# Loading the head of a two-layer kernel in other pieces: second chunk in halves, later x behind it, ten zero matmuls

## The chip, the cores and the metric

The kernel runs on one core of one Trainium2 chip. The metric is the device time of one execution in microseconds (us). Engines are called as the profile calls them: PE is TensorE (PEld its weight loads), DVE VectorE, ACT ScalarE, POOL GpSimd, SP the engine that issues most DMA transfers. All times in this document are us unless marked ns.

## The reference

Eight samples of 256 rows by 1024 features go through two residual layers:

```python
# layer 0: one weight for all, plus a +-1 mask per sample, scaled by a coefficient per sample
output = jnp.einsum('bsi,oi->bso', hidden_states, W) + b
sign = (2 * mask - 1).astype(hidden_states.dtype)
diff = jnp.einsum('bsi,bio->bso', hidden_states, sign)
y = x + output + diff * coeff[:, None, None]
# layer 1: a weight per sample, chosen by id among eight
out = y + jnp.einsum('bsi,boi->bso', y, weight[adapter_ids])
```

x is (8, 256, 1024) in float32, the mask (8, 1024, 1024) in int32, the eight layer-1 weights (8, 1024, 1024) in float32. Since coeff multiplies a whole sample, layer 0 of a sample is one product with the matrix W.T + coeff * (2 * mask - 1).

## The kernel before

**Stages.** One stage is one layer of one sample, in the order (layer, sample) = (0,0), (1,0), (0,1), (0,2), (1,1), (0,3), (1,2) and so on to (1,7). The first stage is called the head. All others compute their 1024 x 1024 product by seven half-size products p1 to p7 (a Winograd scheme, table `PRODUCTS`) on quarter blocks named 11, 12, 21, 22. They need sums of activation blocks (s1 to s4) and of weight blocks (t1 to t4), which DVE makes (`sum_of`, L542 and L559). TensorE's order is p1, p5, p6, p2, p7, p3, p4. p5 multiplies s1 with t1, p6 multiplies s2 with t2, p7 multiplies s3 with t3, p4 uses t4. DVE adds the products into the result (`add`, L672). In a layer-0 stage ACT scales each mask block (L515) and DVE adds W to it (L529, the fold). For a layer-1 stage the result of layer 0 is transposed: DVE transposes 32 x 32 squares (L439) and ACT moves them into place (`move`, L453, 32 moves a sample).

**The head** works otherwise, since no data is there yet. It takes the contraction in eight chunks k of 128 rows. For each chunk SP loads mask0[k] (L283, 128 x 1024, 512 KB) and w0T[k] (L287, the same size); ACT scales the mask (L301), DVE adds w0T to it (L309, the fold), and TensorE multiplies, into four PSUM tiles `first[j, h]`, with column half j of the output (L316, one matmul for each 128 output columns, 256 wide, two records each in the profile). x comes in pairs of chunks (`load_x0`, L274): 256 KB a pair. DVE evicts the four tiles with x and the bias added (L343); that is the input of the next stage, which is computed with weights as the left operand (`flipped`, L598). Stages after that use L608.

What is loaded in one go is a piece. `pieces` lists them: chunk 0 in two column halves, the other chunks whole. `load_w0` puts x of chunks 0 and 1 behind the first piece, of chunks 2 and 3 behind chunk 1, of chunks 4 to 7 behind chunk 2. `parts` says in what spans of columns a piece is scaled and folded: the first piece in quarters of a row's 1024 columns, chunk 1 in halves, others whole. The matmuls of a piece wait only for the span that they read. The last two chunks are multiplied by column half: chunks 6 and 7 for j = 0, then for j = 1, so that half of the output can be evicted sooner.

**What sets the order.** Each load, scale, fold, group of matmuls, sum and addition is a `Task` with an engine, an expected length and what it comes after. `plan` runs a list schedule over these lengths, and each engine's program is written in the order of the planned starts. The lengths of the head's scales and folds follow from `length` (0.4 for the first piece, 0.75 for chunk 1, 1.22 for the others). All head transfers go through SP's one queue in the order of their issue.

**Before the tasks** (L797 to L810), TensorE multiplies zeros: eight matmuls 128 x 512 in bfloat16 into a tile that nobody reads. After the fifth, one small matmul spreads the coefficients over the partitions, and DVE makes c2_sb and cn_sb of them, which the scales use.

Of the kernel before, what the change touches and what calls it, by code (L numbers as in the profile page):

```python
# [14 lines left out]
P = 128  # L15
# [126 lines left out]
def kernel(  # L142
# [26 lines left out]
    nc = tc.nc  # L169
    B = coeff.shape[1]  # L170
    _, _, _, KH, TH = xT.shape
    NL, _, _, _, H = w1T.shape
    KC, D = 2 * KH, 2 * H
# [35 lines left out]
    zeros = const.tile([P, H], BF16, name="zeros")  # L209
# [10 lines left out]
    def task(*args, **kw):  # L220
        tasks.append(Task(*args, **kw))
        return tasks[-1]

    def take(r: Buffer):
        count[0] += 1
        r.tile = pools[r.pool].tile(shapes[r.pool], F32, tag=r.pool, name=f"{r.pool}_{count[0]}")
        return r.tile
# [30 lines left out]
    first = {(j, h): Buffer("ps") for j in range(2) for h in range(2)}  # L258
    xb = Buffer("r")
    half = KH // 2  # L260
    pieces = [(0, ds(0, H)), (0, ds(H, H))] + [(k, ds(0, D)) for k in range(1, KC)]
    w0_rows = w0_sb.rearrange("p k j n -> p k (j n)")

    def x0_view():
        flat = x0.tile.rearrange("p q k n -> p (q k n)")[:, 0 : KC * 2 * TH]
        return flat.rearrange("p (k n) -> p k n", k=KC)
# [5 lines left out]
    def load_x0(lo: int, hi: int, queue):  # L272
        pairs = slice(lo // 2, hi // 2)
        queue.dma_start(  # L274
            out=x0_view()[:, lo:hi].rearrange("p (g k) n -> p g (k n)", k=2),
            in_=x0T[pairs].rearrange("g p n -> p g n"),
        )

    def load_mask(n: int):
        k, cols = pieces[n]  # L280
        if m[k // 2].tile is None:
            take(m[k // 2])
        nc.sync.dma_start(out=m_view(k)[:, cols].bitcast(I32), in_=mask0[k][:, cols])  # L283

    def load_w0(n: int):
        k, cols = pieces[n]
        nc.sync.dma_start(out=w0_rows[:, k, cols], in_=w0T[k][:, cols])  # L287
        if n in (0, 2, 3):
            load_x0(*{0: (0, 2), 2: (2, KH), 3: (KH, KC)}[n], nc.sync)

    def parts(n: int):

        k, cols = pieces[n]
        size = {0: 2 * P, 2: H}.get(n, cols.size)
        return k, [ds(at, size) for at in range(cols.start, cols.start + cols.size, size)]

    def scale_first(n: int):
        k, spans = parts(n)
        for cols in spans:
            t = m_view(k)[:, cols]  # L300
            nc.scalar.activation(  # L301
                t, t.bitcast(I32), AF.Identity, bias=cn_sb[:, 0:1], scale=c2_sb[:, 0:1]
            )

    def fold_first(n: int):
        k, spans = parts(n)
        for cols in spans:
            t = m_view(k)[:, cols]
            v.tensor_tensor(t, t, w0_rows[:, k, cols], ALU.add)  # L309
# [43 lines left out]
    for n, (k, cols) in enumerate(pieces):  # L353
        share = cols.size / D
        opens = opened != k // 2
        length = {0: 0.4, 2: 0.75}.get(n, 1.22 * share)
        ld = task(
            "DMA",
            1.32 * share,
            lambda n=n: load_mask(n),  # L360
            takes=[m[k // 2]] if opens else [],
            uses=[] if opens else [m[k // 2]],
            latency=1.5,
            latest=0.2 * n,
        )
        ld2 = task(
            "DMA", 1.32 * share, lambda n=n: load_w0(n), latency=1.5, latest=0.2 * n + 0.1
        )
        sc = task("ACT", length, lambda n=n: scale_first(n), after=[ld], uses=[m[k // 2]])
        fo = task("DVE", length, lambda n=n: fold_first(n), after=[sc, ld2], uses=[m[k // 2]])  # L370
        folded.append(fo)
        last_scale = sc
        opened = k // 2
        if n == 0:
            tasks[0].takes = [x0] + list(tasks[0].takes)
            tasks[0].uses = [x0] + list(tasks[0].uses)
            x0.users += 1
# [91 lines left out]
    def stage(s: int):  # L469
# [66 lines left out]
        def sum_of(what: str, after=()):  # L536
# [24 lines left out]
            for n, rows in enumerate(parts):  # L561
                t = task(
                    "DVE",
                    BLOCK / len(parts),
                    lambda rows=rows: emit(rows),
                    after=[done[left], done[right], done.get(what), *after],
                    takes=[W[what]] if fresh and n == 0 else [],
                    uses=src + ([W[what]] if fresh and n else []),
                )
                if fresh and n == 0:  # L570
                    t.stage = s
                done[what] = t
# [222 lines left out]
    with tc.manual_schedule():  # L795
        take(x0)
        nc.scalar.dma_start(out=c_row, in_=coeff)  # L797
        v.memset(zeros, 0.0)
        v.memset(ones, 1.0)
        v.memset(warm, 0.0)  # L800

        nc.scalar.activation(warm, warm, AF.Identity, bias=warm, scale=1.0)
        idle = pools["ps"].tile([P, H], F32, tag="ps", name="idle")
        c_ps = pools["ps"].tile([P, B], F32, tag="ps", name="c_ps")
        for n in range(8):
            nc.tensor.matmul(out=idle, lhsT=zeros[:, 0:P], rhs=zeros, start=True, stop=True)
            if n == 4:
                nc.tensor.matmul(out=c_ps, lhsT=ones, rhs=c_row, start=True, stop=True)
                v.tensor_scalar(c2_sb, c_ps, 2.0, None, ALU.mult)
                v.tensor_scalar(cn_sb, c_ps, -1.0, None, ALU.mult)  # L810
        for t in plan(tasks, room, may_take):
            t.emit()
            if t is folded[0]:

                v.memset(ids_sb, 0)
                v.memset(b_sb, 0.0)
                nc.gpsimd.dma_start(out=ids_sb, in_=ids)
                nc.gpsimd.dma_start(out=b_sb, in_=biasT)
# [58 lines left out]
```

## Time and profile before

| what | value |
|---|---|
| time, median of 3 runs | 404.0 us (403.77 to 405.08) |
| the profiled execution's own time | 404.47 us |
| its span, first to last instruction | 402.7 us |
| PE busy | 396.5 us, 98% of the span |
| DVE busy | 330.5 us, 82% |
| ACT busy | 183.5 us, 46% |
| granted TensorE clock, mean | 0.999 |
| moved by DMA | 102.99 MB, mean 256 GB/s |

A group's line in the profile names the source line, the engine, the operation, what is written and read with its shape, the number of instructions, and then busy time, the mean ns of one and the idle time ahead of them with what ended it. A timeline's row has the start, the duration, the engine and the same names, and in brackets the idle time of that engine just before. "SPq" rows are issues of transfers, not the transfers themselves. w is any weight tile, a any activation tile, r a row tile of results, ps a PSUM tile, w_sb the copy of W. In the changed kernel a line stands one lower in the file than in the kernel before (L316 becomes L317), from L803 on some more.

### The profile page before, as it was taken

The numbers are of one execution on the slowest core, as the hardware profiler recorded it, in microseconds if no ns is written. First come the engines' busy times: TensorE is split into PE (matmuls) and PEld (weight loads), VectorE is DVE, ScalarE is ACT, GpSimd is POOL, SyncE is SP. The second block draws the span as 40 slices with busy tenths as digits, with TensorE's granted clock in tenths as the row PEclk, the third lists the DMA queues.
The fourth block names the chain that finished last, engine by engine and source line by source line (L and its number), as shares of the span: only waits on it lengthen the run. The fifth ranks groups of instructions, "written<-read, shape, count | busy, mean of one in ns | idle before, by whom it ended". The sixth has DMA issues, their size and how long they took to land.

```text
span 402.7 us, 3428 instructions
## 1 busy us (share of the span) xinstructions
PE 396.5 (98%) x1154; PEld 201.8 (50%) x1154; DVE 330.5 (82%) x306; ACT 183.5 (46%) x303; POOL 27.2 (7%) x44
## 2 busy tenths in 40 slices
PE   8899999999999999999999999999999999999996
PEld 5689995444444444444444444444444444444443
DVE  2347999999999999799968998789977999668242
ACT  3461735205952396880069610894119920391000
POOL 1000111100011100011010100102001020001101
PEclk9999999999999999999999999999999999999999
DMA  7999999982696828958399583987659694701102
GB/s 268 408 413 422 422 335 400 380 293 107 251 343 194 357 104 341 335 164 319 111 401 304 187 336 112 370 255 282 239 200 338 194 365 157 281 33 53 53 0 105
DMA packets 18564, 102.99 MB, mean 256 GB/s; under 512 B 2226, under 2 KB 2482, under 8 KB 9074
## 3 DMA queue, kind: packets, MB, share of 16 engines
q1 hardware_dynamic: 13952, 87.23, 55.9%
q0 software_dynamic: 4448, 15.47, 14.4%
q8 instruction: 9, 0.15, 0.1%
q14 instruction: 9, 0.07, 0.1%
q10 hardware_dynamic: 146, 0.07, 0.1%
HBM read 94.38 MB, written 8.39 MB: 255 GB/s over the span
## 4 chain that ended last, share of the span: by engine, by line
PE 92%; DMA 4%; DVE 2%; issue 1%; SPq 0%; DVEq 0%
PE ps L608 84%; PE ps L598 5%; DMA w_sb<-w0T 4%; PE ps L316 4%; DVE w L559 1%; DVE a L343 0%; DVE w L309 0%; SPq L283 0%; DVE a L542 0%; SPq L274 0%; SPq L287 0%; DVE r L757 0%; DVEq L343 0%; DVEq L309 0%
## 5 line engine op out<-in xcount | busy, mean ns | idle before, releaser
L608 PE MATMUL ps<-w,a 128*128 128x512 f32 (+1 forms) x792 | 336.7, 588 | 0.0
L608 PEld LDWEIGHTS ps<-w,a 128*128 128x128 f32 x792 | 149.9, 190 | 186.7 <-issue 183.4
L559 DVE TENSOR_TENSOR w<-w,w 128x2048 f32<-128x2048 f32 (+1 forms) x61 | 136.8, 2252 | 3.0 <-PE ps L608 2.5
L453 ACT ACTIVATE a<-turn 32x256 f32<-32x256 f32 x224 | 92.7, 414 | 68.5 <-DVE turn L439 65.7
L672 DVE TENSOR_TENSOR r<-r,ps 128x512 f32<-128x512 f32 x73 | 49.1, 680 | 24.9 <-PE ps L608 24.6
L529 DVE TENSOR_TENSOR w<-w,w_sb 128x2048 f32<-128x2048 f32 x28 | 63.9, 2286 | 5.7 <-ACT w L515 5.7
L515 ACT ACTIVATE w<-w,cn_sb,c_sb 128x2048 f32<-128x2048 int32 x28 | 58.5, 2091 | 15.7 <-DMA w<-mask 15.3
L542 DVE TENSOR_TENSOR a<-a 128x512 f32<-128x512 f32 x59 | 39.4, 686 | 0.3
L644 ACT ACTIVATE s<-ps 128x512 f32<-128x512 f32 x15 | 8.9, 591 | 63.2 <-PE ps L608 54.0
L316 PE MATMUL ps<-a,w 128*128 128x256 f32 x128 | 30.5, 399 | 1.1 <-DVE w L309 1.0
L698 POOL DMA_DIRECT2D out<-r x31 | 17.0, 550 | 190.1 <-DVE r L672 190.0
L316 PEld LDWEIGHTS ps<-a,w 128*128 128x128 f32 x128 | 25.3, 201 | 6.8 <-DVE w L309 3.2
L644 ACT ACTIVATE u<-ps 128x512 f32<-128x512 f32 x15 | 8.9, 595 | 39.2 <-PE ps L608 38.8
L309 DVE TENSOR_TENSOR w<-w,w_sb 128x1024 f32<-128x1024 f32 (+2 forms) x11 | 10.2, 934 | 15.2 <-DMA w_sb<-w0T 12.8
L598 PE MATMUL ps<-a,w 128*128 128x128 f32 x192 | 22.0, 276 | 0.2 <-DVE a L542 0.2
L598 PEld LDWEIGHTS ps<-a,w 128*128 128x128 f32 x192 | 21.8, 192 | 0.5 <-DVE a L542 0.4
L418 POOL DMA_DIRECT2D r<-bias x7 | 8.7, 1245 | 173.9 <-DMA r<-xR 173.9
L439 DVE STREAM_TRANSPOSE turn<-r 128x512 f32<-128x512 f32 x28 | 19.8, 708 | 0.6
L301 ACT ACTIVATE w<-w,cn_sb,c_sb 128x1024 f32<-128x1024 int32 (+2 forms) x11 | 10.9, 1004 | 14.6 <-DMA w<-mask 13.1
L672 DVE TENSOR_TENSOR r<-r,s 128x512 f32<-128x512 f32 x14 | 9.6, 684 | 6.6 <-ACT s L644 6.6
L672 DVE TENSOR_TENSOR r<-r,u 128x512 f32<-128x512 f32 x14 | 9.6, 686 | 3.4 <-ACT u L644 3.4
L343 DVE TENSOR_TENSOR a<-ps,r 128x512 f32<-128x512 f32 x4 | 2.7, 688 | 3.2 <-PE ps L316 3.2
(27 smaller groups left out, 24.8 us busy)
## 6 DMA issues: line engine op xcount, KB each, us to landing
w<-w1T SPq DMA_DIRECT2D x32, 1024.0 KB, 8.4
w<-mask SPq DMA_DIRECT2D x28, 1024.0 KB, 10.0
out<-r POOLq DMA_DIRECT2D x31, 256.0 KB, 7.4
r<-xR SPq DMA_DIRECT2D x7, 1024.0 KB, 8.0
a<-xT SPq DMA_DIRECT2D x7, 1024.0 KB, 9.2
r<-bias POOLq DMA_DIRECT2D x7, 1024.0 KB, 15.7
w<-mask SPq DMA_DIRECT2D x7, 512.0 KB, 9.9
w_sb<-w0T SPq DMA_DIRECT2D x7, 512.0 KB, 10.2
```

Of the source, the lines that this page charges most:

```text
L316: nc.tensor.matmul(out=t.rearrange("p (c n) -> p c n", c=half)[:, c % half], lhsT=m_view(k)[:, ts(oc, P)], rhs=x0_view()[:, k], start=k == ...
L439: lambda t=t, opens=not turned: v.transpose(out=(take(r) if opens else r.tile)[:, t], in_=view(source.tile)[:, 2 * t + j]),
L453: nc.scalar.activation(to[:, :, :, f], src[:, :, :, g], AF.Copy)
L515: nc.scalar.activation(t, t.bitcast(I32), AF.Identity, bias=cn_sb[:, b : b + 1], scale=c2_sb[:, b : b + 1])
L529: lambda q=q: v.tensor_tensor(W[q].tile, W[q].tile, w0[q], ALU.add),
L542: lambda: v.tensor_tensor(part(what), part(left), part(right), op),
L559: v.tensor_tensor(to[:, rows], a, c, op)
L598: nc.tensor.matmul(out=t[:, ts(c, TH)], lhsT=W[w].tile[:, k, ts(c, P)], rhs=part(a)[:, k], start=opens and c == 0 and k == 0, stop=k == KH ...
L608: nc.tensor.matmul(out=t[:, cols], lhsT=part(a)[:, k], rhs=W[w].tile[:, k, cols], start=opens and k == 0, stop=k == KH - 1, skip_group_che ...
L644: lambda: nc.scalar.activation(take(r), bank.tile, AF.Copy),
L672: v.tensor_tensor(to, left, get(r), op)
L698: lambda: (queue or nc.gpsimd).dma_start(out=out0[:, block(q)] if flipped else out[b - 1, :, int(q[0]) - 1, lo:hi], in_=R[b].tile[:, block ...
```

## The change

Chunk 1 is loaded in two column halves, as chunk 0 is, so there is one piece more. x of chunks 2 and 3 stays behind chunk 1, now behind its second half; x of chunks 4 to 7 goes behind chunk 3 instead of chunk 2. `parts` and `length` have an entry for one piece beside the first; its number goes from 2 (then chunk 1) to 4 (now chunk 2), so that chunk 1's halves are scaled and folded one by one as they come, and chunk 2 is scaled and folded in two halves. In `plan`'s input a half of chunk 1 has half of 1.22, chunk 2 has 0.75. Ahead of the head TensorE multiplies zeros ten times, the last two 256 and 128 columns wide.

```diff
-    pieces = [(0, ds(0, H)), (0, ds(H, H))] + [(k, ds(0, D)) for k in range(1, KC)]
+    pieces = [(k, ds(j * H, H)) for k in range(2) for j in range(2)]
+    pieces += [(k, ds(0, D)) for k in range(2, KC)]
...
     def load_w0(n: int):
         k, cols = pieces[n]
         nc.sync.dma_start(out=w0_rows[:, k, cols], in_=w0T[k][:, cols])
-        if n in (0, 2, 3):
-            load_x0(*{0: (0, 2), 2: (2, KH), 3: (KH, KC)}[n], nc.sync)
+        if n in (0, 3, 5):
+            load_x0(*{0: (0, 2), 3: (2, KH), 5: (KH, KC)}[n], nc.sync)
...
-        size = {0: 2 * P, 2: H}.get(n, cols.size)
+        size = {0: 2 * P, 4: H}.get(n, cols.size)
...
-        length = {0: 0.4, 2: 0.75}.get(n, 1.22 * share)
+        length = {0: 0.4, 4: 0.75}.get(n, 1.22 * share)
...
-        for n in range(8):
-            nc.tensor.matmul(out=idle, lhsT=zeros[:, 0:P], rhs=zeros, start=True, stop=True)
+        for n, size in enumerate((H, H, H, H, H, H, H, H, 2 * P, P)):
+            nc.tensor.matmul(
+                out=idle[:, 0:size], lhsT=zeros[:, 0:P], rhs=zeros[:, 0:size], start=True, stop=True
+            )
             if n == 4:
```

Here P is 128, H 512, D 1024, KH 4 and KC 8.

## The prediction

> **What bounds the kernel now.** I read the page's busy row first, then the chain that ended last, then the timelines of TensorE, the DMA queue and VectorE over the first 47 us.
>
> The page's first row and, from the chain in order of time (start us, us, what), its pieces after 18 us:
>
> ```profile
> PE 396.5 (98%) x1154; PEld 201.8 (50%) x1154; DVE 330.5 (82%) x306; ACT 183.5 (46%) x303; POOL 27.2 (7%) x44
> ...
> 7.49 10.63 DMA w_sb<-w0T
> 18.22 1.24 DVE w L309
> 19.50 14.10 PE ps L316 x64
> ...
> 40.08 0.70 DVE a L542
> 40.83 21.70 PE ps L598 x192
> 62.53 336.52 PE ps L608 x792
> ```
>
> TensorE runs without a break from 40.83 to 399.05. So only two things shorten the run: TensorE reaching 40.83 earlier, and nothing later running out because of it. Ahead of that the chain is a transfer (chunk 3 of w0T, issued at 7.49, landed by 18.12), its fold, and matmuls. TensorE's timeline, with idle time in brackets:
>
> ```profile
> 5.49 5.54 PE L316 MATMUL ps<-a,w 128*128 128x256 f32 x16
> 11.81 7.50 PE L316 MATMUL ps<-a,w 128*128 128x256 f32 x32 [0.78 <-DVE w L309]
> 19.50 17.53 PE L316 MATMUL ps<-a,w 128*128 128x256 f32 x80 [0.19 <-DVE w L309]
> 36.87 3.73 PE L598 MATMUL ps<-a,w 128*128 128x128 f32 x32
> 40.83 10.98 PE L598 MATMUL ps<-a,w 128*128 128x128 f32 x96 [0.22 <-DVE a L542]
> ```
>
> A chunk is 16 records. From 19.50 to 36.87, 80 records take 17.37: 0.216 each, and 0.10 more for the first after a wait; a chunk is 3.45. The 32 records at 36.87 go at 0.112 each (21.70 / 192 = 0.113), so TensorE could have gone on at 40.44 and not at 40.83: 0.39 lost, plus 0.10 for the restart. The idle column understates these waits, since ends are modelled.
>
> The DMA queue of SP. Its waits are landings: an issue stands until the transfer eight before it has landed, so each start here dates a landing:
>
> ```profile
> 12.95 0.33 SPq L287 DMA_DIRECT2D w_sb<-w0T  x1
> 14.23 0.33 SPq L283 DMA_DIRECT2D w<-mask  x1
> 15.58 0.33 SPq L287 DMA_DIRECT2D w_sb<-w0T  x1
> 16.86 0.33 SPq L283 DMA_DIRECT2D w<-mask  x1
> 18.14 0.33 SPq L287 DMA_DIRECT2D w_sb<-w0T  x1
> ```
>
> In order these are the landings of mask 2, w0T 2, x of chunks 4-7, mask 3, w0T 3. VectorE's folds start with them (14.30, 18.22), ScalarE's scales too (12.95, 16.87). The head is bound by the order and the bytes of this queue until TensorE, at 3.45 a chunk against 2.56 of transfer, falls behind it at 19.50.
>
> VectorE between head and stage 1:
>
> ```profile
> 33.69 0.69 DVE L343 TENSOR_TENSOR a<-ps,r 128x512 f32<-128x512 f32 x1 [0.17 <-PE ps L316]
> 34.29 4.55 DVE L559 TENSOR_TENSOR w<-w,w 128x1024 f32<-128x1024 f32 x3
> 38.76 1.28 DVE L343 TENSOR_TENSOR a<-ps,r 128x512 f32<-128x512 f32 x2
> 40.08 0.69 DVE L542 TENSOR_TENSOR a<-a 128x512 f32<-128x512 f32 x1
> ```
>
> The three L559 are t1 in halves and t3. t3 (2.29) stands ahead of the last two evictions and s1, and s1 is what p5 waits for at 40.83.
>
> **The change, part by part.**
>
> (1) Chunk 1 in halves. Two transfers of 512 KB become four of 256 KB, with rows of 2 KB instead of 4 KB. Two more issues on SP at 0.43 each: SP is far ahead of the data (w0T 3 is issued at 7.49 and lands at 18.12), so they cost nothing; without that cover, 0.9. Eight transfers in flight now hold fewer bytes, but near 9.7 still 2.75 MB (three of 256 KB, four of 512 KB), at 512 KB in 1.28 some 7 us of work: the engines don't run dry. The rows cost something: 512 KB of x in 2 KB rows took 15.58 - 14.23 = 1.35, 512 KB in 4 KB rows 1.28. So +0.07 per 512 KB, and chunk 1 (1 MB) delays all behind it by 0.14. [...] TensorE is through with chunk 0 at about 11.1; the first half of chunk 1 is folded by about 10.4 (w0T 1 landed by 11.0, less two transfers of 0.65), the second by 11.9, so chunk 1 ends near 14.7, ahead of chunk 2 and not a bound.
>
> (2) Chunk 2 is now the one that is scaled and folded in halves (size table of `parts`). Its first fold starts at 14.30 + 0.14 = 14.44. Chunk 1 shows today what a half is worth: fold at 11.06, matmul at 11.81, 0.75 later. So chunk 2 begins at 15.19 instead of 15.58. The second half follows 0.61 later, when TensorE has 1.8 of work. ScalarE's extra instruction (0.81 and about 0.7 against 1.24) ends before w0T 2 lands.
>
> (3) x of chunks 4-7 moves behind chunk 3: 1.35 earlier for chunk 3, less 0.14. Fold 18.22 - 1.21 = 17.01, matmul 19.50 - 1.21 = 18.29. TensorE is on chunk 2 until 15.19 + 0.10 + 3.45 = 18.74, so no wait. That x now lands at about 18.3, and is read from 22.2.
>
> (4) What is late next: chunk 4, whose bytes are only delayed by the 0.14. Fold 20.78 + 0.14 = 20.92, matmul 1.28 later, 22.20. TensorE is done with chunk 3 at 18.74 + 3.45 = 22.19: a dead heat. Before, it came to chunk 4 at 19.50 + 0.10 + 3.45 = 23.05. The head gains 0.85. Chunks 5-7 are folded 0.9 and more ahead of TensorE. Stage 1 starts at 36.02 instead of 36.87.
>
> (5) The order. SP's and POOL's lists are as before outside the head. The planner, fed the new lengths, puts t3 behind s1, t2, s2 and one addition on VectorE. First evictions 0.85 earlier, at 31.97 and 32.83; t1 needs the second w1 block (landed 33.45, now 33.59), so t1 runs 33.63 to 36.0; evictions 35.9 and 36.5, s1 37.1 to 37.8. p5 is wanted at 36.02 + 3.57 = 39.59: the wait of 0.39 + 0.10 goes, with 1.8 to spare. t2 and s2 end at 40.0 and 40.7, p6 begins at 43.2; t3 ends near 43.5, p7 begins at 50.3.
>
> (6) Two short zero matmuls (and two weight loads beside them). Cold ones of 512 columns are spaced 0.43, so these take 0.21 and 0.11. Today the eighth leaves TensorE free at 5.22, and 5.49 is the fold; now free at about 5.55. 0.06 later, covered by the 0.78 of waiting at 11.81. What they do to the clock is not in the trace. The first eight records of L316 take 634 ns each, those from 9.4 on 379:
>
> ```profile
> L316 PE MATMUL ps<-a,w x8: 634/634/767, 5.5 to 8.6; 128*128 128x256 f32 x8
> ...
> L316 PE MATMUL ps<-a,w x7: 379/379/380, 9.4 to 10.6; 128*128 128x256 f32 x7
> ```
>
> Full speed came 3.7 us after 5.49. An earlier release gains nothing, chunk 2's data being the bound. [...]
>
> **Sum.** 0.85 + 0.49 = 1.34 us less.
>
> **Does the rest follow?** TensorE comes 1.34 earlier to everything after 41 us. VectorE is nearly full from 33 to 100 us and gains less at once, but it waits 0.9 for TensorE at 69.44, which absorbs that. In the next stretch the new order puts the addition of p7 ahead of a fold and waits about 0.6 for it; from there it is some 0.8 ahead. The tightest place is the second layer of the second sample at 110.44: ScalarE's moves (L453) end at 109.42, a margin of 1.0. Now 108.6 against 109.1: 0.5 left. p5 and p6 of the stage at 86.4 have over 1 us each. If this cover goes, part of 1.34 is given back, not more.
>
> The profiled execution took 404.47, span 402.7, so 1.8 lies outside; it stands 0.5 above the median of 404.0, within their spread of 403.77 to 405.08. I take the 1.34 off the median: 402.7.
>
> **Rivals.** *(a) Part of it only.* If the half of chunk 2 doesn't let TensorE start, chunk 2 begins at 15.72 and the head gains 0.33, in all 0.82: 403.2. If p5 still waits, 0.85: 403.15. [...] If the moves at 109 are late by more than 0.5, the same sort of size. For: the dead heat in (4). Against: the row of chunk 1, and 1.8 of spare time for s1.
> [...]
> *(c) Nothing arrives.* If some wait later had bound TensorE anyway, 404.0; the unbroken 358 us speak against it.
>
> **Numbers.** What a measurement of this kernel can tell from no change is about 0.3%, 1.2 us; 402.8 is the border. The forecast is 0.68 (its own range 402.2 to 403.1; 0.58 of it beyond the border, 0.10 short of it), (a) and (c) together 0.20 (0.02 beyond the border), (b) and other losses 0.12. So faster 0.60, same 0.28, slower 0.12. The range 401.9 to 404.2 takes in (a), (c), and leaves out most of (b).
>
> **What would show it.** Span about 401.4. L316 after the first 32 records without a pause from 15.2; chunk 2's first fold near 14.4; chunk 3's near 17.0; L598 starting near 36.0, and no gap ahead of its second 32; L608 starting near 61.0. Wrong if chunk 2's fold comes past 15.2, if L316 pauses near 22, or if L608 shows a wait near 109.

## The result, and the profile after

| | before | after |
|---|---|---|
| median | 404.2 us (403.77 to 405.08, 7 runs) | 402.83 us (402.45 to 403.55, 7 runs) |
| ratio, 95% interval | | 0.9963 (0.9952 to 0.9975) |
| profiled execution, its span | 404.47, 402.7 us | 403.55, 401.8 us |

The changed kernel is faster by 1.5 us (404.2 x 0.0037), with an interval of 1.0 to 1.9; the medians lie 1.37 apart. The predicted time was 402.7. The execution that was profiled is the slowest of the seven (their spans go from 400.7 to 401.8), so its trace shows less of the gain than the median has: 0.9 of span.

The page of the changed kernel, its busy row and the chain that ended last (start us, us, what):

```profile
PE 396.2 (99%) x1156; PEld 202.5 (50%) x1156; DVE 330.9 (82%) x307; ACT 183.8 (46%) x304; POOL 27.2 (7%) x44
...
1.68 4.84 DMA a<-x0T
6.52 0.14 issue
6.65 30.12 PE ps L317 x128
36.77 25.01 PE ps L599 x224
61.78 336.52 PE ps L609 x792
```

No fold and no DVE step is left in the chain. It is one transfer, the first pair of x, and from 6.65 on nothing but TensorE. The last piece has the same 336.52 as before, so all that was gained lies ahead of it. TensorE's timeline:

```profile
3.97 1.78 PE L807 MATMUL idle<-zeros 128*128 128x512 bf16 x5
6.65 30.12 PE L317 MATMUL ps<-a,w 128*128 128x256 f32 x128 [0.90 <-DMA a<-x0T]
36.61 14.46 PE L599 MATMUL ps<-a,w 128*128 128x128 f32 x128
```

Before, the 128 head records stood in three rows with waits at 11.81 and 19.50; now they are one row. Stage 1 starts at 36.61 (36.87 before), and its p5 follows p1 without a gap: 128 records in one row, where before 32 and 96 stood apart. p5 starts at 36.61 + 3.57 = 40.18 (40.83 before). The head gave 0.26, the wait of p5 0.39, its restart 0.10: 0.75, and stage 2 starts at 61.62 instead of 62.37. What else the span lost, 0.14, lies behind TensorE's last matmul.

SP's queue. The waiting issues date landings: the first three those of a mask half, a w0T half and a mask half, the last five those of mask 2, w0T 2, mask 3, w0T 3 and x of chunks 4 to 7, in this order:

```profile
7.28 0.33 SPq L288 DMA_DIRECT2D w_sb<-w0T  x1
7.92 0.33 SPq L284 DMA_DIRECT2D w<-mask  x1
8.57 0.33 SPq L288 DMA_DIRECT2D w_sb<-w0T  x1
...
12.64 0.33 SPq L288 DMA_DIRECT2D w_sb<-w0T  x1
13.92 0.33 SPq L284 DMA_DIRECT2D w<-mask  x1
15.20 0.33 SPq L288 DMA_DIRECT2D w_sb<-w0T  x1
16.48 0.33 SPq L284 DMA_DIRECT2D w<-mask  x1
17.83 0.33 SPq L288 DMA_DIRECT2D w_sb<-w0T  x1
```

Chunk 2 landed at 13.92 (14.23 before), chunk 3 at 16.48 (18.14 before). VectorE, from the fold of chunk 2 on:

```profile
14.02 1.29 DVE L310 TENSOR_TENSOR w<-w,w_sb 128x512 f32<-128x512 f32 x2 [2.56 <-DMA w_sb<-w0T]
16.56 1.23 DVE L310 TENSOR_TENSOR w<-w,w_sb 128x1024 f32<-128x1024 f32 x1 [1.25 <-DMA w_sb<-w0T]
20.47 1.22 DVE L310 TENSOR_TENSOR w<-w,w_sb 128x1024 f32<-128x1024 f32 x1 [2.68 <-DMA w_sb<-w0T]
...
34.04 2.35 DVE L560 TENSOR_TENSOR w<-w,w 128x1024 f32<-128x1024 f32 x2
36.30 1.28 DVE L344 TENSOR_TENSOR a<-ps,r 128x512 f32<-128x512 f32 x2
37.62 0.69 DVE L543 TENSOR_TENSOR a<-a 128x512 f32<-128x512 f32 x1
...
41.64 2.28 DVE L560 TENSOR_TENSOR w<-w,w 128x2048 f32<-128x2048 f32 x1
```

The two halves of t1 at 34.04, the last two evictions, s1 at 37.62; t3 only at 41.64. s1 was at 40.08 before, behind t3.

Why did so early data give the head only 0.26? Two rows of the records of L317 (how many; least, median and largest duration in ns; from when to when):

```profile
L317 PE MATMUL ps<-a,w x10: 634/634/765, 6.7 to 10.6; 128*128 128x256 f32 x10
```

```profile
L317 PE MATMUL ps<-a,w x116: 379/379/471, 11.1 to 36.0; 128*128 128x256 f32 x116
```

TensorE started late, at 6.65, since the first x landed at 6.52 (5.36 before), and its first ten records went at the slow clock (634 ns each; by the trace's clock record full speed came at 11.2). The trace has the starts of slow records 0.427 apart and those of fast ones 0.216, so the head can be written as a sum: start + 128 x 0.216 + 0.211 for each slow record + the rest. Here 6.65 + 27.65 + 2.11 + 0.20 = 36.61. The rest is what the first three terms leave over: the waits, with 0.10 for each restart after one and about 0.13 that the first record takes longer. Here no wait is left in it, and the end is set by the start and the clock. The same sum over every profiled execution of this study (kernels as told below; stage 1 is the end of the sum; p5 less stage 1 is 3.57 where p5 does not wait):

| kernel | first matmul | slow records | rest (waits) | stage 1 starts | p5 less that |
|---|---|---|---|---|---|
| before | 5.49 | 8 | 2.04 | 36.87 | 3.96 |
| after | 6.65 | 10 | 0.20 | 36.61 | 3.57 |
| e1_t3_late | 7.00 | 9 | 0.20 | 36.74 | 3.57 |
| e2_x_only | 5.46 | 10 | 0.60 | 35.82 | 5.00 |
| e3_halves_only | 6.72 | 0 | 2.20 | 36.57 | 3.57 |
| e4_eight_zeros | 5.99 | 12 | 0.14 | 36.31 | 3.57 |
| e5_x_and_t3 | 5.46 | 4 | 2.00 | 35.95 | 3.57 |
| e6_after_t3_early | 5.46 | 0 | 2.64 | 35.75 | 4.83 |
| e7_x_first | 7.26 | 8 | 0.12 | 36.71 | 3.57 |
| e8_x_act | 5.69 | 0 | 2.13 | 35.47 | 3.57 |
| e9_chunk2_whole | 6.41 | 0 | 2.04 | 36.10 | 3.57 |
| e10_thirds_x_act | 5.64 | 9 | 0.29 | 35.48 | 3.57 |
| e11_few_zeros | 5.20 | 13 | 0.19 | 35.79 | 3.57 |
| e12_thirds_few_zeros | 5.68 | 14 | 0.12 | 36.40 | 3.57 |

Rows with a rest of 2 us and more are bound by the data, rows with 0.1 to 0.3 by TensorE's own start and clock; e2, with 0.60, stands between.

### The profile page after: what moved, and what is told of

Read it like the earlier page. It is cut to its first block, busy times and chain, and to the rows that moved or that the text cites. A ratio compares the mean times of both kernels' runs of the same rounds, so it can differ in the third digit from the quotient of the medians.

```text
span 401.8 us, 3435 instructions
## 1 busy us (share of the span) xinstructions
PE 396.2 (99%) x1156; PEld 202.5 (50%) x1156; DVE 330.9 (82%) x307; ACT 183.8 (46%) x304; POOL 27.2 (7%) x44
## 4 chain that ended last, share of the span: by engine, by line
PE 97%; DMA 1%; SPq 0%; issue 0%; DVE 0%
PE ps L609 84%; PE ps L317 7%; PE ps L599 6%; DMA a<-x0T 1%; SPq L288 0%; SPq L284 0%; DVE r L758 0%
## 5 line engine op out<-in xcount | busy, mean ns | idle before, releaser
L317 PE MATMUL ps<-a,w 128*128 128x256 f32 x128 | 30.1, 401 | 0.9 <-DMA a<-x0T 0.9
L317 PEld LDWEIGHTS ps<-a,w 128*128 128x128 f32 x128 | 25.9, 203 | 5.1 <-DVE b_sb L819 1.2
L310 DVE TENSOR_TENSOR w<-w,w_sb 128x512 f32<-128x512 f32 (+2 forms) x12 | 10.3, 869 | 14.9 <-DMA w_sb<-w0T 10.8
L302 ACT ACTIVATE w<-w,cn_sb,c_sb 128x512 f32<-128x512 int32 (+2 forms) x12 | 11.2, 953 | 13.9 <-DMA w<-mask 12.4
L807 PE MATMUL idle<-zeros 128*128 128x512 bf16 (+2 forms) x10 | 4.1, 575 | 1.2 <-DVE zeros L799 1.2
```

Of the source, the lines that this page charges most:

```text
L317: nc.tensor.matmul(out=t.rearrange("p (c n) -> p c n", c=half)[:, c % half], lhsT=m_view(k)[:, ts(oc, P)], rhs=x0_view()[:, k], start=k == ...
```

## The experiments

Each kernel was timed against the kernel before in five rounds, e1 to e4 and e12 on one chip, e5 to e11 on another; the median of before was 404.12 to 404.30 in each of these comparisons. The intervals are about 0.001 wide to each side, 0.4 us, so two kernels have to differ by about 0.5 before they count as different.

### The two links one by one

**e1_t3_late**: the kernel before, t3 of the first flipped stage put behind t2 by hand, nothing else.

```diff
-            sum_of("t3")
+            sum_of("t3", [done["t2"]])
```

> The kernel before with one edit: in stage 1, t3 comes after t2 in the task graph, so that VectorE's order in stage 1 becomes that of the changed kernel; queue, pieces and zero matmuls stay. Theory (order): the wait of p5 at 40.83 goes, 0.39 + 0.10 = 0.49 us less, the head unchanged (stage 1 still begins near 36.9), time about 0.1% below before. Rival (the head alone gives the gain): no change in time, p5 waits for something else, such as the second evictions.

Measured: 403.59 us, ratio 0.9983 (0.9974 to 0.9992), 0.7 us less. TensorE's timeline:

```profile
7.00 29.91 PE L316 MATMUL ps<-a,w 128*128 128x256 f32 x128 [1.57 <-DMA a<-x0T]
36.74 14.46 PE L598 MATMUL ps<-a,w 128*128 128x128 f32 x128
```

p5 follows p1 without a wait (3.57). So the order on VectorE is worth something by itself; the 0.49 of the prediction lies inside its interval (0.3 to 1.1). Its head is the head of the kernel before, yet ran with a rest of 0.20 instead of 2.04, since x landed late in this execution (first matmul 7.00) and the clock was slow for nine records: 36.74, no later than 36.87. In these two traces of the old head a start 1.5 later cost nothing, because the waits for data took it up.

**e2_x_only**: the kernel before, x of chunks 4 to 7 behind chunk 3, nothing else.

```diff
-        if n in (0, 2, 3):
-            load_x0(*{0: (0, 2), 2: (2, KH), 3: (KH, KC)}[n], nc.sync)
+        if n in (0, 2, 4):
+            load_x0(*{0: (0, 2), 2: (2, KH), 4: (KH, KC)}[n], nc.sync)
```

> The kernel before with x of chunks 4 to 7 behind chunk 3 instead of chunk 2, nothing else; VectorE's order is that of before. Theory (queue order): chunk 3 is folded 1.35 earlier, TensorE goes from chunk 2 to chunk 3 without a wait at 19.14 instead of 19.50, stage 1 begins 0.46 earlier, p5 still waits 0.39, in all 0.46 less (0.1%). Rival (TensorE's start bounds the head): the head gains only what the first matmul's start allows, so 0.46 or nothing from one execution to the next; if the first matmul comes past 6.5, chunk 2 itself is late and stage 1 begins no earlier than before.

Measured: 404.02 us, ratio 0.9997 (0.9991 to 1.0004): nothing that can be told from no change. The expectation of 0.46 missed. TensorE's timeline of e2 and VectorE's:

```profile
35.82 3.73 PE L598 MATMUL ps<-a,w 128*128 128x128 f32 x32
40.82 10.98 PE L598 MATMUL ps<-a,w 128*128 128x128 f32 x96 [1.26 <-DVE a L542]
```

```profile
34.13 4.71 DVE L559 TENSOR_TENSOR w<-w,w 128x1024 f32<-128x1024 f32 x3 [0.80 <-DMA w<-w1T]
...
40.07 0.69 DVE L542 TENSOR_TENSOR a<-a 128x512 f32<-128x512 f32 x1
```

The head is 1.05 earlier (35.82): 0.58 of it because chunk 2 happened to land earlier in this execution (TensorE came to it at 15.00 instead of 15.58), and 0.47 from there on, which is the expected 0.46. But p5 stands where it stood (40.82 against 40.83). t1 now waits for the landing of the second w1 block (0.80 idle ahead of 34.13), which the change doesn't move; t3 follows in the same row, and s1 is at 40.07 again. The whole gain of the head becomes wait of p5: 40.82 - 35.82 - 3.57 = 1.43 instead of 0.39.

**e3_halves_only**: the changed kernel with x of chunks 4 to 7 back behind chunk 2, and eight zero matmuls.

```diff
-        if n in (0, 3, 5):
-            load_x0(*{0: (0, 2), 3: (2, KH), 5: (KH, KC)}[n], nc.sync)
+        if n in (0, 3, 4):
+            load_x0(*{0: (0, 2), 3: (2, KH), 4: (KH, KC)}[n], nc.sync)
```

> The changed kernel with x of chunks 4 to 7 back behind chunk 2 and eight zero matmuls: the halves of chunks 1 and 2, and VectorE's new order. Theory (queue order): chunk 2 begins at about 15.2, but chunk 3's fold comes 0.14 later than before, 18.36, so TensorE stands still for about 0.8 ahead of chunk 3 and begins it at 19.64; the head loses 0.14, p5's wait is gone (-0.49), in all 0.35 less. Rival (smaller pieces alone carry the head's gain): stage 1 begins 0.8 earlier, 1.3 less.

Measured: 403.48 us, ratio 0.9985 (0.9977 to 0.9994), which can't be told from e1: what the halves by themselves show in the time is the planner's new order. TensorE comes to chunk 2 at 14.80 and then stands at chunk 3, which is still behind x:

```profile
19.20 17.54 PE L317 MATMUL ps<-a,w 128*128 128x256 f32 x80 [0.67 <-DVE w L310]
```

**e5_x_and_t3**: the edits of e1 and of e2 together, no halves, eight zeros.

> The two edits of the earlier runs together and nothing else: x of chunks 4 to 7 behind chunk 3, and t3 after t2; pieces as before, eight zero matmuls. Theory (a chain of two links: the head's gain reaches p5 only when t3 is out of s1's way): stage 1 near 35.8 to 36.7 by when the first x lands, p5 right behind p1 at 39.4 to 40.3, in all 1.0 to 1.5 less than before, near the changed kernel; the halves and short zeros give less than 0.4. Rival (the halves of chunks 1 and 2 carry the head's gain): like t3 alone, 0.6 less.

Measured: 403.29 us, ratio 0.9977 (0.9969 to 0.9984), 0.9 us less; stage 1 at 35.95, no wait at p5. By the medians the two moves, without halves or added zeros, bring 0.83 of the 1.37. Whether halves and zeros add the other 0.54 is not shown: the interval overlaps that of the changed kernel.

**e6_after_t3_early**: the changed kernel with t3 put ahead of t2 and s1 again.

```diff
             sum_of("t1")
-            sum_of("t2", got)
             sum_of("t3")
+            sum_of("t2", [*got, done["t3"]])
```

> The changed kernel with t3 put ahead of s1 and t2 again in stage 1 (behind the second evictions). Theory (two links): s1 ends 2.2 later, near 40.5, p5 begins near 40.6 wherever stage 1 began, and nearly all the gain is lost: 0 to 0.3 less than before. Rival (the head alone matters): as the changed kernel, 1.4 less than before.

Measured: 403.86 us, ratio 0.9988 (0.9978 to 0.9998). The changed kernel loses 1.0 us of its gain (0.0025 of 404.2). TensorE and VectorE of e6:

```profile
14.85 21.06 PE L317 MATMUL ps<-a,w 128*128 128x256 f32 x96 [0.42 <-DVE w L310]
35.75 3.73 PE L599 MATMUL ps<-a,w 128*128 128x128 f32 x32
40.57 10.98 PE L599 MATMUL ps<-a,w 128*128 128x128 f32 x96 [1.09 <-DVE a L543]
```

```profile
34.16 2.36 DVE L560 TENSOR_TENSOR w<-w,w 128x1024 f32<-128x1024 f32 x2 [0.90 <-DMA w<-w1T]
...
37.63 2.28 DVE L560 TENSOR_TENSOR w<-w,w 128x2048 f32<-128x2048 f32 x1
39.83 0.69 DVE L543 TENSOR_TENSOR a<-a 128x512 f32<-128x512 f32 x1
```

Stage 1 starts at 35.75, 1.12 earlier than before; t3 at 37.63 holds s1 back to 39.83, and p5 starts at 40.57, only 0.26 earlier. Together the runs make a table, medians less that of before in the same comparison (us):

| | t3 ahead of s1 | t3 behind s1 |
|---|---|---|
| head as before | 0 | -0.58 (e1) |
| x moved | -0.15 (e2) | -0.83 (e5) |
| x moved, halves, ten zeros | -0.26 (e6) | -1.37 (after) |

Going down the left column brings 0.26, down the right one 0.79. Each entry is uncertain by about 0.4, so the medians alone do not show that the two parts fail to add (e1 and e2 make 0.73 together, e5 0.83). The traces show it: with t3 ahead of s1 a head that ended 1.05 and 1.12 earlier moved p5 by 0.01 and 0.26.

### The zeros and TensorE's start

**e4_eight_zeros**: the changed kernel with the eight zero matmuls of before.

> The changed kernel without the two short zero matmuls (eight as before). Theory (the data bound the head, zeros are free): the same time as the changed kernel, 0.3% below before. Rival (the clock counts: in the profile after, TensorE never pauses in the head, so each cold matmul is on the path): the release of the clock comes later in some executions and the time is up to 0.6 us more than the changed kernel's; the 634 ns records last past 11 us.

Measured: 403.25 us, ratio 0.9976 (0.9963 to 0.9989). The median gains 0.45 less than that of the changed kernel, but half of the changed kernel's interval (0.9952 to 0.9975) lies inside this one; what the two short ones are worth is not shown. In its profile twelve records were slow, two more than in that of after.

**e7_x_first**: the changed kernel, the first pair of x first in SP's queue instead of third.

```diff
+        load_x0(0, 2, nc.sync)
...
-        if n in (0, 3, 5):
-            load_x0(*{0: (0, 2), 3: (2, KH), 5: (KH, KC)}[n], nc.sync)
+        if n in (3, 5):
+            load_x0(*{3: (2, KH), 5: (KH, KC)}[n], nc.sync)
```

> The changed kernel with x of chunks 0 and 1 as the very first transfer, ahead of mask and w0T of chunk 0. Theory (data of chunk 4 bound the head): nothing changes, the same bytes are in before chunk 4; within 0.2 of the changed kernel. Rival (TensorE's first matmul bounds the head: it came at 6.65 with x the last to land, and TensorE never paused after): x lands first, the first fold follows 0.65 later than 4.98, the first matmul comes near 6.1 and no longer swings with x; up to 0.5 less than the changed kernel.

Measured: 403.07 us, ratio 0.9970 (0.9957 to 0.9982): no gain over the changed kernel. The first matmul was at 7.26. Now the first piece of w0T was third in the queue, and it landed at 6.65. Where x is third, it landed at 5.36 in the profile of before, 6.52 in that of after, 6.87 in e1, 5.23 in e2, 6.58 in e3, 5.86 in e4, 5.22 in e5, 5.33 in e6, 6.28 in e9, 5.07 in e11. So the place in the queue is late at times, whichever of the two tensors it holds.

**e8_x_act**: the same line taken out of `load_w0`, and that pair issued on ACT's queue, behind c_row.

```diff
+        load_x0(0, 2, nc.scalar)
```

> The changed kernel with x of chunks 0 and 1 issued on ScalarE's queue behind the coefficients, beside mask and w0T of chunk 0 on SP's. Theory (data of chunk 4): within 0.2 of the changed kernel. Rival (TensorE's first matmul): x is no longer last, the first matmul comes by 6.0, up to 0.5 less than the changed kernel.

Measured: 402.55 us, ratio 0.9960 (0.9945 to 0.9975); not to be told from the changed kernel by its interval. Its profile shows a data-bound head, as no record was slow (and SP's queue carried one transfer less):

```profile
5.69 1.99 PE L317 MATMUL ps<-a,w 128*128 128x256 f32 x8
8.67 5.45 PE L317 MATMUL ps<-a,w 128*128 128x256 f32 x24 [0.99 <-DVE w L310]
14.58 21.06 PE L317 MATMUL ps<-a,w 128*128 128x256 f32 x96 [0.46 <-DVE w L310]
```

From chunk 2, at 14.58, TensorE is never stopped for long, and stage 1 starts at 35.47. At chunk 4 it is close: the fold ended at 21.50, and TensorE came to the chunk at 21.59.

**e11_few_zeros**: the changed kernel with five zero matmuls of 128 columns in place of the ten.

```diff
-        for n, size in enumerate((H, H, H, H, H, H, H, H, 2 * P, P)):
+        for n, size in enumerate((P, P, P, P, P)):
```

> The changed kernel with five zero matmuls of 128 columns in place of the ten. Theory (data bound the head): at most 0.2 more than the changed kernel. Rival (the cold clock is on the path): the release comes only after the first full stretch of matmuls, past 9 in every execution, chunk 2 begins at 15.5 to 16.5, and the time is 0.5 to 1.0 above the changed kernel's.

Measured: 402.69 us, ratio 0.9966 (0.9953 to 0.9979). The loss of 0.5 to 1.0 that the rival expected did not come. TensorE's timeline:

```profile
2.07 0.56 PE L811 MATMUL c_ps<-c_row,ones 1*128 1x8 f32 x2 [0.16 <-DMA c_row<-coeff]
5.20 30.75 PE L317 MATMUL ps<-a,w 128*128 128x256 f32 x128 [2.57 <-DMA a<-x0T]
```

Without the zeros 13 records were slow, three more than in the profile of after, at 0.211 each: 0.63. But the small matmul for the coefficients, which stands behind five zeros on TensorE, ran at 2.07 instead of 3.45, so the first fold came 0.4 earlier (at 4.57 instead of 4.98). The zeros hold up the very chain whose matmuls they are meant to speed up.

### Further versions

**e9_chunk2_whole**: the changed kernel with chunk 2 scaled and folded whole.

```diff
-        size = {0: 2 * P, 4: H}.get(n, cols.size)
+        size = {0: 2 * P}.get(n, cols.size)
```

> The changed kernel with chunk 2 scaled and folded whole (chunk 1 in halves, x moved, ten zero matmuls, VectorE's new order all kept). Theory (chunk 2's data bound the head when the first x lands early and the clock is released early): chunk 2 begins 0.5 later in such executions, near 15.1 instead of 14.6, and the median is 0.3 to 0.5 above the changed kernel's. Rival (TensorE's start and cold clock bound the head in most executions, as in the profile after): no difference, the half is not read before it is there.

Measured: 403.05 us, ratio 0.9973 (0.9964 to 0.9982). In its profile, where no record was slow, chunk 2 starts 1.28 after its fold (15.28, folded from 14.00), against 0.75 in e6 (14.85, from 14.10) and in e8 (14.58, from 13.83): 0.53 for folding chunk 2 in halves where the data is the bound. In the time it is 0.4 by the ratios and 0.1 by the medians less those of before, inside the intervals.

**e10_thirds_x_act**: e8, and chunk 2 also loaded in halves, chunk 3 scaled and folded in halves (the numbers of the pieces that x and `length` go by move with them).

```diff
-    pieces = [(k, ds(j * H, H)) for k in range(2) for j in range(2)]
-    pieces += [(k, ds(0, D)) for k in range(2, KC)]
+    pieces = [(k, ds(j * H, H)) for k in range(3) for j in range(2)]
+    pieces += [(k, ds(0, D)) for k in range(3, KC)]
...
-        size = {0: 2 * P, 4: H}.get(n, cols.size)
+        size = {0: 2 * P, 6: H}.get(n, cols.size)
```

> Meant to beat the changed kernel: x of chunks 0 and 1 on ScalarE's queue (as before), chunk 2 also loaded in halves, chunk 3 folded in halves. If chunk 2's data bind when the clock is free: chunk 2 begins near 13.5 instead of 14.6, chunk 3 near 17.0, stage 1 near 34.9 instead of 35.5, s1 ends near 37.8 ahead of p5 at 38.5, 0.5 less than with x on ScalarE's queue alone, in all 2.0 less than before. If TensorE's start and clock bind: the same as with x on ScalarE's queue alone.

Measured: 402.43 us (402.3 to 402.55), ratio 0.9956 (0.9943 to 0.9969), the lowest median of the study and, in five executions, the narrowest scatter, though the interval overlaps that of the changed kernel. Nine records were slow and the rest was 0.29: stage 1 at 35.48, where e8 with none slow and a rest of 2.13 had 35.47. Its one stop is at the last chunk, folded until 30.14 and begun at 30.19: 0.2, restart included.

**e12_thirds_few_zeros**: e10 with the five short zeros of e11.

> The last candidate (x of the first pair on ScalarE's queue, chunks 1 and 2 in halves, chunk 3 folded in halves) with five zero matmuls of 128 columns in place of the ten. In its profile TensorE ran unbroken from 5.64 although the clock was released at 9.5 only, and with few zeros the changed kernel began at 5.20 since the scales came 0.4 earlier. If the start counts: first matmul near 5.2, stage 1 at 35.0 to 35.5, up to 0.4 less than the last candidate. If a late release counts more: release past 9 in every execution, stage 1 at 35.5 to 35.9, the same or 0.3 more.

Measured: 402.7 us, ratio 0.9960 (0.9947 to 0.9974), no better than e10. The start did not come earlier (5.68): with x on ACT's queue the first fold waits for w0T, at 5.21, 5.16 and 5.20 in e8, e10 and e12, so earlier scales bring nothing. And 14 records were slow against 9: 5 x 0.211 = 1.06, of which 0.92 is seen in stage 1 (36.40 against 35.48).

## Why the prediction was right, and which steps were not

**The time.** 402.7 was predicted, 402.83 measured, by the two links that the prediction named: the head's data and p5's wait. The interval of 1.0 to 1.9 leaves out the 0.82 and 0.85 that the variants of rival (a) would have saved. That the sum came out so close is partly chance, as the terms show.

**(1) Halves of chunk 1: right that they are cheap.** The transfers of chunk 2 were to land 0.14 later and landed 0.31 earlier, but that is scatter. By the issues behind it, w0T of chunk 2 landed at 13.64 to 14.23 in the four profiles with chunk 1 whole (before, e1, e2, e5) and at 13.73 to 14.24 in the six with halves and x on SP's queue as in the changed kernel (after, e3, e4, e6, e9, e11): 0.14 can't be told from nothing. A queue made late by the smaller transfers, the (b) among the chances, shows in no run: in the queue of this profile issues that wait for halves of 256 KB stand 0.65 apart (7.28, 7.92, 8.57) and those that wait for 512 KB 1.28 apart (12.64, 13.92, 15.20, 16.48); in the profile of before two issues that wait for 256 KB stood 0.65 apart too (6.84, 7.49).

**(2) and (3) Chunks 2 and 3: the times were right within half a microsecond.** Chunk 2's first fold was to start at 14.44 and started at 14.02, chunk 3's at 17.01 and started at 16.56. The 0.75 from a half's fold to its matmul came out in e6 and e8. So in this execution the data would have let chunk 2 begin at 14.02 + 0.75 = 14.77 instead of the predicted 15.19, 0.4 earlier, because it landed earlier.

**(4) The dead heat at chunk 4 did not come in this execution.** Its fold started at 20.47, and TensorE came to it at 22.80. L317 has no pause near 22. The head ended at 36.61 in this execution and not at 36.02: 0.26 gained and not 0.85. The cause is in (6), not in the data. Where start and clock were kind, the head gained 1.1 (e6, with the changed kernel's loads) and 1.4 (e8), and there the dead heat came: in e6 the fold ended at 21.77 and TensorE took up the chunk at 21.86.

**(5) The order: right in mechanism and place.** s1 was expected from 37.1 to 37.8 and ran at 37.62; t3 was to end near 43.5 and ended at 43.92; the wait of 0.39 and the restart of 0.10 went. What the step lacked is what the order is worth once the head is earlier. The prediction priced the head at 0.85 and the order at 0.49 as if either could be had alone. By the medians of e2 and e6 the head alone is worth 0.15 to 0.26 (the first can't be told from nothing), since t1 then waits for w1 and t3 keeps s1 at 39.8 to 40.1. With the earlier head the order is worth 1.0 (after against e6).

**(6) TensorE's start and clock: the step that failed.** The first real matmul was taken at 5.55, and the clock's effect at 0, "chunk 2's data being the bound". The first matmul came at 6.65, for the landing of x and not for the zeros, and with ten slow records TensorE reached chunk 2 at 15.89, past its data (folded from 14.02). From a data-bound chunk 2 to stage 1 e6 took 35.75 - 14.85 = 20.90, so by an estimate the data of this execution would have let the head end at 14.77 + 20.90 = 35.67: 1.20 earlier than before, of which start and clock took 0.94 and left 0.26. Full speed, read at 5.49 + 3.7 = 9.2 in the profile of before, came at 11.2 here (the last slow record starts at 10.6), and at 4.7 to 7.4 in e3, e5, e6, e8 and e9. Start and clock were read from one profiled execution as if they were properties of the kernel. The landing of the first x, third in the queue, fell anywhere from 5.1 to 6.9 in ten profiles. In the head before, that scatter was invisible: its 2.04 of waits took it up (e1 against before). The change took the waits away and laid the scatter open in the head. So the head gained anything from 0.26 (after) to 1.12 (e6) with the changed kernel's loads, and 1.4 in e8. The median's 1.37 less 0.49 for p5 leaves 0.88 for it, and 0.85 was predicted: if that split holds, the loss left out here and data that landed earlier than taken in (2) made up for each other, which is luck.

That the other six executions have spans 0.4 to 1.1 shorter than the profiled one fits this, but only one execution has a trace, so it is argued and not shown. The time of the whole run does not show the wider scatter either: seven executions of before lie 1.31 apart, seven of the changed kernel 1.10.

**The rest of the run: right.** The margin of the moves was to fall to 0.5. They now end at 109.30:

```profile
98.68 10.62 ACT L454 ACTIVATE a<-turn 32x256 f32<-32x256 f32 x25
```

and the layer that reads them starts at 110.44 - 0.75 = 109.69: 0.39 left, and TensorE has no wait from 36 us to the end. The prediction had them at 108.6; they moved less than TensorE did, as it feared, and just enough here.

**Rival (a)**, with 0.82 or 0.85 left of the gain, comes near the profiled execution, which gained 0.75, though what took the rest there was TensorE's start and clock; the forecast describes the median. **Rival (c)** is refuted for the whole change, but it is exactly what happens to half of it: e2.

**What stays open.** What the halves and the two short zeros add to the time; whether e10 beats the changed kernel; why the third transfer lands between 5.1 and 6.9.

## What to carry to other kernels

An earlier start counts only if what the next consumer waits for is freed too: before pricing a gain in one stage, follow the first wait of the next stage back to what it would then be bound by (here a landing that the change doesn't move, and a long sum in front of a short one), and look at what a list scheduler reorders on the way. Write the stretch as start + work at full clock + slow records + waits; when the waits reach zero, the next gain is in the start and the clock, and in the profiles here these scattered, in kernels with the same loads and zeros too. A transfer's landing in one profile is a sample: where a forecast rests on it, its scatter belongs in the range.

## What the runs showed of the hardware that was not expected

By the clock records of the fourteen traces, full speed came between 4.7 us (e3) and 11.8 us (e12) after the start of the span, in kernels whose zero matmuls are alike too: 11.3 with eight zeros (e4), 4.7 with the same eight (e3), 5.2 (e8) and 11.2 (after) with ten. Zeros ahead of the work don't settle it; with hardly any (e11, e12) it was 11.0 and 11.8.

Transfers of 256 KB in rows of 2 KB took half the time of 512 KB in rows of 4 KB, behind one another in one queue: in the profile of after the issues that wait for them stand 0.65 apart (7.28, 7.92, 8.57) and 1.28 apart (12.64, 13.92, 15.20, 16.48). The third transfer of the program scattered by 1.8 us (landed at 5.07 to 6.87), yet the next one, x late or early, landed at 6.8 to 7.5 in the ten profiles with x third: the queue as a whole was not late.

With x issued on ACT's queue beside SP's, what SP loads at that time came later: the first piece of w0T landed at 5.03 to 5.09 in e8, e10 and e12, and at 4.28 to 4.71 in the ten profiles with x third in SP's queue.
